# Decoder layer in float32: two more pairs of feed-forward blocks multiplied by two levels of seven products, and the weight preparation spread anew

## The chip, the cores and the metric

One core of a Trainium2 chip runs the whole layer in one launch. The metric is the device time of a launch in microseconds (us); for the kernel before it is the median of three runs.

## The reference, cut to what matters

```
x = x + attn(layernorm(x))            # one head of width 256, over each batch's 128 rows
x = x + xattn(layernorm(x), ctx)      # 8 linear-attention heads of width 64
h = layernorm(x)                      # 16 batches x 128 rows, width 1024
W = (nibble(Wq) - zero) * scale       # int4 weights, groups of 64; gate, up: 2752x1024, down: 1024x2752
x = x + (silu(h @ Wg.T) * (h @ Wu.T)) @ Wd.T
```

Everything is float32. The 2048 rows go through the feed-forward in two passes of 1024.

## The kernel before, in words

**Order of the work.** Self-attention (four groups of four batches, loop `for t in range(NT)`), cross-attention (16 batches), the feed-forward's first pass over gate and up, its second pass, and the down projection. All of it is one program; what isn't marked as kept in program order may be moved by the scheduler that builds each engine's instruction list. What goes through `InOrder` (line 53) keeps the order in which the code issues it.

**Seven products instead of eight.** The 2752 hidden units make 11 blocks of 256 (the last, number 10, has 192; `RB` is 10). A block's product of weights (256x1024) by activations (1024x1024 tokens) is cut into halves in all three dimensions and formed from seven products in place of eight (Strassen's scheme in Winograd's form). The seven left operands per matrix are sums of quarters of the dequantised weights; `prepare` (line 200) makes them on VectorE and stores them in DRAM. The right operands, called T, are sums of quarters of the activations and are made once per pass.

**One level**, `one_block` (line 1108), used for blocks 0 to 9 in the first pass: `SEQUENCE` has seven products for gate and seven for up. A product is four matmuls of 128x128 weights by 128x512 activations (`products`, line 1070, tile `p`). ScalarE copies three of the partial sums out (`k`), VectorE adds them (`sg`, `h`), and `h` is stored. PSUM banks are shared by several products: product 3 is accumulated in the bank that the sum for product 5 has just been read from, so it must wait until VectorE has read that one.

**Two levels**, `two_levels` (line 1279), used in the second pass for all five pairs of blocks: each of the seven outer products of a pair is itself formed from seven inner ones. The matmuls are 128x128 by 128x256 (tile `q`). One outer step is 7 inner products of 4 matmuls, for gate and up and both blocks at once. GpSimd forms four inner left operands (`li`) per outer step from two loaded weight tiles, VectorE forms four inner right operands (`ti`, `inner_right`, line 1228) and adds up the outer sums U, V and C (`got`, line 1325); ScalarE copies (`k`) and applies silu. Five of the seven sets of right operands are kept for all pairs (`KEPT`). VectorE's small jobs that aren't sums are queued in `soon_due` and `extra` and issued by `do_extra` (line 1291) between products.

**Preparing weights.** `prepare` is a generator. A matrix of a block takes three steps: two units (each loads 256 KB of packed weights and their scales and zeros, then six VectorE instructions on tiles `pa`) and one combination (four VectorE instructions on tiles `pc`); seven tiles of 256 KB are stored. Loads run two units ahead. Here the first three blocks' gate and up (18 steps) are prepared in self-attention (`EARLY = 3`, one load ahead), in groups 1 and 2. The other 79 steps run from block 0 of the first pass on: `beside` (line 1475) takes one step after 9 of a block's 14 products, with gate, up and down jobs mixed (`attention_done`, line 972).

**Loads and stores.** Nearly all DMAs are issued by SyncE in one queue. `load_weights` (line 1007) fetches prepared weights as tiles of 512 KB, four tiles ahead, from the list `to_load`; a tile buffer comes free when TensorE has used it. The second pass's activations (`b`, 4.2 MB) are loaded ahead of block 8.

Of the kernel before, what the change touches and what calls it, by code (L numbers as in the profile page):

```python
# [18 lines left out]
P = 128  # L19
# [46 lines left out]
def decoder_layer(  # L66
# [214 lines left out]

    EARLY = 3

# [26 lines left out]
    with (  # L310
# [166 lines left out]
        for t in range(NT):  # L477
# [14 lines left out]
            for f in range(4):  # L492
                if t == 0:
                    query_key(f, xnT, qkT, halves[f], ts(1, TB // 2))
                else:
                    query_key(f, xnT, qkT)
                add_bias(t * BPT + f)
                if more:
                    if oT is not None:
                        give((t - 1) * BPT + f, oT)  # L500
                    turn((t + 1) * BPT + f, xnTs[0])
                if more and t > 0:
                    for _ in range(1 + f % 2):
                        next(early, None)
# [15 lines left out]
            oT = attend(atT, v)  # L520
            if more and t > 0:
                for _ in range(3):
                    next(early, None)
    for _ in early:
# [437 lines left out]
    with ExitStack() as gs:  # L962
# [9 lines left out]
        def attention_done():  # L972

            nonlocal cxb, rest
            sides.close()
            prep_pools(second, "f", 6, 2)
            jobs = []
            for blk in range(EARLY, len(BLOCKS)):
                jobs += [(blk, mat) for mat in ("gu" if blk < RB else "rm")]
                if blk >= EARLY + 2:  # L980
                    jobs.append((blk - EARLY - 2, "d"))
            jobs += [(blk, "d") for blk in range(len(BLOCKS)) if (blk, "d") not in jobs]
            rest = prepare(jobs, 2, nc.sync, vector)
            banks.append(pool("c_u", 4, space=PSUM, side="right"))
            cxb = pool("c_xb", 1)

# [8 lines left out]
        def tiles_of(blk):  # L995
            todo = [(blk, *k) for k in (SEQUENCE if blk < RB else LAST)]
            return [todo[n : n + 2] for n in range(0, len(todo), 2)]

        OUTERS = [(i, q) for i in range(NI) for q in DOWN]
        to_load = deque(  # L1000
            [t for blk in range(len(BLOCKS)) for t in tiles_of(blk)]
            + [[(2 * i + f, mat, q) for mat in "gu"] for i, q in OUTERS for f in range(2)]
            + tiles_of(RB)
        )
        loaded, waiting = deque(), deque()
# [63 lines left out]

        def products(T, got):  # L1070

# [6 lines left out]
            def product(q):  # L1078
# [7 lines left out]
                for j in range(JC):  # L1086
                    nc.tensor.matmul(  # L1087
                        ps,
                        wt[:, j, :],
                        T[q][:, j, :],  # L1090
                        start=(first == q and j == 0),
                        stop=(q in (2, 3, 4) and j == JC - 1),
                        skip_group_check=True,
                    )
# [13 lines left out]
        def one_block(blk, T, between):  # L1108
# [20 lines left out]

            make = {"g": products(T, gate), "u": products(T, up)}  # L1130
            for n, (mat, q) in enumerate(SEQUENCE):
# [3 lines left out]
        def last_block(ps, T, between):  # L1135
# [24 lines left out]
            def half_product(p, w, q, start, stop):  # L1160
                for j in range(JC):
                    nc.tensor.matmul(  # L1162
                        bank[p],
# [61 lines left out]
        HT = TB // 2  # L1225
        R = {}

        def inner_right(T, q):

            if q in KEPT and (q, 7) in R:  # L1230
                return []

            def t(kc, h):
                return T[q][:, ts(kc, CHUNKS), ts(h, HT)]

            R[q, 1], R[q, 2], R[q, 3] = t(0, 0), t(1, 0), t(1, 1)

            def comb(k):
                if k == 5:
                    tag = KEPT.get(q, "ti")  # L1240
                    pool = {"ti": deep_pool, "X4": [xres]}.get(tag, [xlate])[0]
                    R[q] = pool.tile([P, 4, CHUNKS, HT], F32, name="ti", tag=tag, bufs=1)
                dst = R[q, k] = R[q][:, (5, 6, 7, 4).index(k)]
                a, b = {
                    5: (t(0, 1), t(0, 0)),
                    6: (t(1, 1), R.get((q, 5))),
                    7: (t(1, 1), t(0, 1)),
                    4: (t(1, 0), R.get((q, 6))),
                }[k]
                vector.tensor_tensor(dst, a, b, ALU.subtract)  # L1250

            return [lambda k=k: comb(k) for k in (5, 6, 7, 4)]

        def inner_left(L, pool, tag):
# [9 lines left out]
            def comb(k):  # L1264
                t = L[k] = pool.tile([P, 2, CHUNKS, P], F32, name="li", tag=tag)
                a, b, op = {
# [8 lines left out]

        deep_pool = []
        deep = ExitStack()

        def two_levels(T):
            scalar = InOrder(tc, nc.scalar)  # L1280
            deep_pool.append(
                deep.enter_context(
                    tc.tile_pool(name="c_d", bufs=1, side="right", reuse_waits="tile")
                )
            )
            wide = [P, 4, 2, HT]


            soon_due, extra = deque(), deque()

            def do_extra(n, more=0):
                for todo, k in ((soon_due, n), (extra, more)):
                    for _ in range(min(k, len(todo))):
                        todo.popleft()()
# [5 lines left out]
            def multiply(n, p):  # L1300
# [3 lines left out]
                if set_ == p:  # L1304
                    bank[p] = banks[n % 2].tile([P, 2, HT], F32, name=f"q{p}", tag="gu")
                ps = bank[set_]
                for m in range(2):
                    for c in range(CHUNKS):
                        tensor.matmul(
                            ps[:, m, :],  # L1310
                            L[p][:, m, c, :],
# [6 lines left out]
                if p in (1, 7, 6):  # L1318
                    t = state[n]["kept"][p] = ct.tile(
                        [P, 2, HT], F32, name="k", tag=f"k{p}", bufs=2 if p == 1 else 1  # L1320
                    )
                    scalar.copy(t, ps)
                put_stores()
# [27 lines left out]
            def finish(i, q):  # L1351
# [5 lines left out]
                def mult(f):  # L1357
# [3 lines left out]
                    hs[s, half, f] = t = t.rearrange("p h t -> p (h t)")  # L1361
                    if s == 1:
                        store(2 * i + f, 4, half, t)
# [20 lines left out]
            def prepare_outer(n):  # L1384
                state[n] = {"L": {}, "bank": {}, "kept": {}}

                state[n]["left"] = inner_left(
                    state[n]["L"], *((chc, "hc") if n == 0 else (ct, "sg"))
                )

# [5 lines left out]
            for n, (i, q) in enumerate(OUTERS):  # L1396
                last = n + 1 == len(OUTERS)
                if q in (1, 5):
                    sums["U" if q == 1 else "V"] = deep_pool[0].tile(
                        wide, F32, name="U" if q == 1 else "V"  # L1400
                    )
# [5 lines left out]
                multiply(n, 6)  # L1407
                do_extra(2)
                if q not in (1, 5):
                    sums["C"] = deep_pool[0].tile(wide, F32, name="C")  # L1410
                if not last:
                    soon_due.extend(inner_right(T, OUTERS[n + 1][1]))
                if n == 0:
                    extra.append(lambda: outer_operand(T, 4))
                elif n == 4:
                    extra.extend(inner_right(T, 4))
                multiply(n, 2)
                got(n, (0, 0), 2, 1)
                do_extra(1)
                multiply(n, 5)  # L1420
# [13 lines left out]
                if not last:  # L1434
                    left(3)
                do_extra(1, 1)
                load_weights()
                if not last:
                    do_extra(len(soon_due))
                    multiply(n + 1, 7)  # L1440
                if q in (2, 3, 7, 4):
                    finish(i, q)


                if q == 3:
                    while extra:
# [4 lines left out]
                elif q == 1 and i > 0 or last:  # L1451
                    do_extra(len(soon_due), len(extra))
                    hl = load_first(i if last else i - 1, 0)
                    combine(i if last else i - 1, 0, hl)
                del state[n]
            return extra

        def load_first(i, half):
# [7 lines left out]
            return hl  # L1466

        for n in range(AHEAD):

            load_weights(nc.gpsimd if n == 0 else nc.sync)  # L1470
        T = T0
        T.update({1: blocks[0, 0], 2: blocks[1, 0], 3: blocks[1, 1]})
        T1 = {}

        def beside(n, mat, q):
            if rest is None:
                tick()
                if not pend:
                    attention_done()
            elif n % 7 in (0, 2, 4, 5) or n == 6:  # L1480
                next(rest, None)

            if blk == RB:
                for k in {("r", 0): (5,), ("r", 1): (7,), ("m", 6): (6,)}.get((mat, q), ()):
                    outer_operand(T1, k)
                if (mat, q) == ("m", 1):
                    for step in inner_right(T1, 1):
                        step()

        for blk in range(len(BLOCKS)):  # L1490
            if blk == RB - 2:
                pass1 = new_blocks(cxb, lambda k: f"b{k}")
                for _ in block_loads(1, pass1):
                    pass
                T1.update({1: pass1[0, 0], 2: pass1[1, 0], 3: pass1[1, 1]})
            if blk == RB:
                blocks.update(pass1)
                last_block(0, T, beside)
            else:
                one_block(blk, T, beside)  # L1500
        for _ in rest:
            pass
        second.close()
        chc = pool("c_hc", 8)
        remaining = two_levels(T1)

# [271 lines left out]
```

## Time and profile before

| what | value |
|---|---|
| runs | 2294.47, 2295.57, 2297.4 us, median 2295.57 |
| profiled execution | 2296.27 us; span from first to last instruction 2294.5 us |
| granted TensorE clock | 0.999 |
| self-attention | 0 to 252 us |
| cross-attention | 252 to about 825 us, its end interleaved with block 0 |
| first pass, blocks 0 to 9, from 808.0 us | until the last block at 1313.6 us |
| first pass, last block | 1313.6 to 1354.8 us |
| second pass, five pairs by two levels | 1354.8 to 1779.9 us |
| second pass, last block, then the down projection | 1779.9 to 1817.6, to 2294.5 us |
| busy: TensorE, VectorE, ScalarE, GpSimd | 2269.7, 1554.0, 555.4, 389.2 us |

PE is TensorE, PEld its weight loads, DVE VectorE, ACT ScalarE, POOL GpSimd, SP SyncE. A row of instructions gives the line in the code, the engine, the operation, the tiles written and read, and their shapes; a bracket gives the idle time before it and what ended it. A line L62 is the helper that keeps the order, so tiles tell such rows apart. One float32 matmul leaves two MATMUL records. A row of a window gives the busy time of each engine in that stretch, the number of instructions in parentheses, the granted clock, the mean busy share of the 16 DMA engines and their rate.

### The profile page before, as it was taken

To read this page: it belongs to the slowest core of one execution; us is meant where nothing else is said; L and a number is where in the kernel's file an instruction comes from. 1 tells how busy PE (TensorE), PEld (TensorE's weight loads), DVE (VectorE), ACT (ScalarE), POOL (GpSimd) and SP (SyncE) were. 2 spreads that over 40 slices of the span, in tenths; PEclk is the share of its full clock that TensorE was granted. 3 is DMA by queue.
4 is the path that set the end of the run, shared out by engine and by line. 5 is a ranking of instruction groups with operands and counts; after the bars stand their busy time and mean duration, and the time that the engine had idled before them with its cause. 6 is when DMAs were issued, how large, how long until landed. Compare 5 with 4: busy or idle time off the path is not lost.

```text
span 2294.5 us, 25166 instructions
## 1 busy us (share of the span) xinstructions
PE 2269.7 (99%) x8928; PEld 1581.6 (69%) x8928; DVE 1554.0 (68%) x2210; ACT 555.4 (24%) x887; POOL 389.2 (17%) x283
## 2 busy tenths in 40 slices
PE   8999999999999999999999999999999999999999
PEld 7556566666666664444444468888888588888888
DVE  6694788788788836677776548777777655444463
ACT  2111256665665652111111111222121100000000
POOL 5120122222222210000000024444443000000000
PEclk9999999999999999999999999999999999999999
DMA  6242356566576657888789733654654974434631
GB/s 245 62 138 90 110 156 184 164 193 189 161 229 203 171 157 249 264 273 281 260 282 332 256 104 103 202 173 140 202 183 145 328 243 153 140 125 148 221 115 37
DMA packets 274797, 425.19 MB, mean 185 GB/s; under 512 B 26225, under 2 KB 119793, under 8 KB 274545
## 3 DMA queue, kind: packets, MB, share of 16 engines
q1 hardware_dynamic: 254192, 396.06, 54.5%
q10 hardware_dynamic: 18016, 18.62, 2.6%
q0 software_dynamic: 2464, 8.91, 1.0%
q8 instruction: 71, 1.16, 0.2%
q14 instruction: 54, 0.43, 0.1%
HBM read 265.62 MB, written 157.35 MB: 184 GB/s over the span
## 4 chain that ended last, share of the span: by engine, by line
PE 94%; DVE 3%; DMA 1%; issue 1%; ACT 0%; SPq 0%; POOL 0%; DVEq 0%; POOLq 0%; ACTq 0%
PE p L1087 23%; PE po L1663 21%; PE q L62 18%; PE mm L62 11%; PE kq L62 8%; PE mm L392 5%; PE tr L62 3%; PE mm L407 2%; PE mm L288 2%; PE p L1162 1%; PE tr L339 1%; DMA kh<-kd 1%; DVE bnst L62 0%; DVE qden L62 0%; DMA wo_again<-in_wo 0%
## 5 line engine op out<-in xcount | busy, mean ns | idle before, releaser
L1087 PE MATMUL p<-b,w 128*128 128x512 f32 x704 | 310.4, 592 | 0.7 <-DMA w<-wg 0.7
L1087 PEld LDWEIGHTS p<-b,w 128*128 128x128 f32 x704 | 133.4, 190 | 167.1 <-issue 162.8
L1087 PE MATMUL p<-T,w 128*128 128x512 f32 x528 | 234.2, 592 | 0.0
L62 PE MATMUL q<-ti,li 128*128 128x256 f32 x840 | 193.0, 379 | 1.0 <-DVE ti L62 1.0
L1087 PEld LDWEIGHTS p<-T,w 128*128 128x128 f32 x528 | 100.1, 190 | 124.6 <-issue 123.1
L1663 PE MATMUL po<-wc,lc 128*128 128x256 f32 x840 | 183.4, 379 | 0.0
L62 POOL TENSOR_TENSOR li<-w 128x512 f32<-128x512 f32 x70 | 96.1, 1374 | 514.6 <-DMA w<-wu 476.8
L62 PEld LDWEIGHTS q<-ti,li 128*128 128x128 f32 x840 | 159.2, 190 | 23.8 <-issue 1.7
L1663 PEld LDWEIGHTS po<-wc,lc 128*128 128x128 f32 x840 | 159.6, 190 | 21.8
L708 POOL TENSOR_TENSOR qe<-qe,qden 128x1024 f32<-128x1024 f32 x64 | 121.6, 1900 | 266.3 <-DVE qden L62 233.6
L62 ACT COPY k<-q 128x512 f32<-128x512 f32 x105 | 61.4, 585 | 324.8 <-PE q L62 324.8
L62 DVE TENSOR_TENSOR pa<-pa,sz 128x512 f32<-128x512 int32 (+1 forms) x172 | 129.0, 750 | 5.4
L1663 PE MATMUL po<-wq,lq 128*128 128x256 f32 x560 | 126.7, 379 | 0.0
L62 PE MATMUL mm<-kh,cxt 128*128 128x256 f32 x512 | 123.0, 383 | 3.3 <-DMA kh<-kd 3.1
L62 PE MATMUL kq<-cx,wk_sb 128*128 128x512 f32 x256 | 122.0, 599 | 3.5 <-ACT ke L665 3.5
L62 PEld LDWEIGHTS mm<-qs,m_sb 128*128 128x128 f32 x512 | 97.2, 190 | 38.9 <-issue 28.0
L62 PE MATMUL kq<-wq_sb,xn 128*128 128x512 f32 x256 | 120.4, 593 | 0.0
L62 PE MATMUL mm<-qs,m_sb 128*128 128x256 f32 x512 | 120.3, 379 | 0.0
L62 PEld LDWEIGHTS mm<-kh,cxt 128*128 128x128 f32 x512 | 96.1, 190 | 33.6 <-issue 18.5
L62 DVE TENSOR_REDUCE qmx<-kq 128x16 f32<-128x1024 f32 x64 | 76.3, 1193 | 63.0 <-PE kq L62 62.8
L1663 PEld LDWEIGHTS po<-wq,lq 128*128 128x128 f32 x560 | 106.0, 190 | 15.7 <-issue 0.9
L392 PE MATMUL mm<-xnT,wqkv_sb 128*128 128x512 f32 (+1 forms) x320 | 113.2, 510 | 0.0
(189 smaller groups left out, 3651.9 us busy)
## 6 DMA issues: line engine op xcount, KB each, us to landing
w<-wu SPq DMA_DIRECT2D x140, 256.0 KB, 3.5
lq<-h SPq DMA_DIRECT2D x140, 256.0 KB, 4.4
w<-wg SPq DMA_DIRECT2D x138, 256.0 KB, 3.0
kd<-kt SPq DMA_DIRECT2D x64, 512.0 KB, 3.5
kh<-kd SPq DMA_DIRECT2D x128, 256.0 KB, 5.6
h<-hc SPq DMA_DIRECT2D x80, 256.0 KB, 2.8
wq<-wd SPq DMA_DIRECT2D x70, 256.0 KB, 5.0
h<-h SPq DMA_DIRECT2D x60, 256.0 KB, 3.2
```

Of the source, the lines that this page charges most:

```text
L62: return lambda *args, **kw: self._tc.keep_in_program_order(fn(*args, **kw))
L288: tensor.matmul(ps, oT[:, d, ts(b % BPT, S)], wo_d[d][:, ts(h, 512)], start=(d == 0), stop=(d == 1),)
L339: nc.tensor.transpose(tr[:, j, :], xn[:, ts(4 * h + j, P)], ident)
L392: nc.tensor.matmul(ps[:, tokens], wqkv_sb[:, f, c, :], xnT[:, c, tokens], start=(c == 0), stop=(c == CC - 1),)
L407: nc.tensor.matmul(ps, xnT[:, c, ts(i, S)], wqkv_sb[:, 4:6, c, :], start=(c == 0), stop=(c == CC - 1),)
L708: nc.gpsimd.tensor_tensor(qe, qe, den.unsqueeze(2).to_broadcast(wide), ALU.mult)
L1087: nc.tensor.matmul(ps, wt[:, j, :], T[q][:, j, :], start=(first == q and j == 0), stop=(q in (2, 3, 4) and j == JC - 1), skip_group_check= ...
L1162: nc.tensor.matmul(bank[p], w[:, j, :], T[q][:, j, :], start=(start and j == 0), stop=(stop and j == JC - 1), skip_group_check=True,)
L1663: nc.tensor.matmul(bank[:, i, :], l[:, ts(i, S)], w,  start=(start and c == 0 and i % 2 == 0), stop=(stop and c == len(pairs) - 1), skip_g ...
```

## The change

In the first pass blocks 4 to 7 (pairs 2 and 3) go through `two_levels` between block 3 and block 8. That function now takes the pass, the pairs and an object that holds a pass's right operands. In the first pass nothing is kept: all seven sets are made for each of the two pairs, in two buffers. The order in which the four inner right operands of a set are made is 7, 5, 6, 4 instead of 5, 6, 7, 4, in the second pass too, and they have a queue of their own, `right`. Five blocks are prepared in self-attention (30 steps, now in all four groups) instead of three. The other 67 steps are 12 per one-level block (after all products but n = 3 and 10), 9 in block 3, one per pair in the two-level part, and 5 in the last block; all of gate and up comes first, then down. The second pass's activations are loaded after the two-level part. TensorE's products from block 1 on are kept in program order.

```diff
-    EARLY = 3
+    EARLY = 5
...
-                if more and t > 0:
+                if t > 0:
                     for _ in range(1 + f % 2):
                         next(early, None)
...
-            if more and t > 0:
-                for _ in range(3):
-                    next(early, None)
+            for _ in range((4, 3, 3, 2)[t]):
+                next(early, None)
...
-            jobs = []
-            for blk in range(EARLY, len(BLOCKS)):
-                jobs += [(blk, mat) for mat in ("gu" if blk < RB else "rm")]
-                if blk >= EARLY + 2:
-                    jobs.append((blk - EARLY - 2, "d"))
-            jobs += [(blk, "d") for blk in range(len(BLOCKS)) if (blk, "d") not in jobs]
+            jobs = [(blk, mat) for blk in range(EARLY, RB) for mat in "gu"]
+            down = [(blk, "d") for blk in range(len(BLOCKS))]
+            jobs += down[:4] + [(RB, "m"), (RB, "r")] + down[4:]
...
+        PAIRS = [2, 3]
+        order = [blk for blk in range(RB) if blk // 2 not in PAIRS]
+        order.insert(2 * PAIRS[0], None)
...
-            return [lambda k=k: comb(k) for k in (5, 6, 7, 4)]
+                return [lambda k=k: comb(k) for k in (7, 5, 6, 4)]
...
                 multiply(n, 6)
-                do_extra(2)
+                do_extra(len(right))
+                while soon_due:
+                    soon_due.popleft()()
...
-                    soon_due.extend(inner_right(T, OUTERS[n + 1][1]))
+                    right.extend(operands.inner_right(OUTERS[n + 1][1]))
...
                 got(n, (0, 0), 2, 1)
-                do_extra(1)
                 multiply(n, 5)
...
                     hs[s, half, f] = t = t.rearrange("p h t -> p (h t)")
-                    if s == 1:
+                    if ps == 0:
+                        store(2 * i + f, 1 + s, half, t)
+                    elif s == 1:
                         store(2 * i + f, 4, half, t)
...
-            elif n % 7 in (0, 2, 4, 5) or n == 6:
+            elif {2 * PAIRS[0] - 1: n < 9, RB: n % 2 == 0}.get(blk, n % 7 != 3):
                 next(rest, None)
...
-        for blk in range(len(BLOCKS)):
-            if blk == RB - 2:
+        for blk in order:
+            if blk is None:
+                two_levels(
+                    0, PAIRS, first_operands, lambda q: q == 1 and next(rest, None)
+                )
+                deep.close()
+                cxb = pool("c_xb", 1)
                 pass1 = new_blocks(cxb, lambda k: f"b{k}")
```

## The prediction

> **What bounds the kernel now.** The page comes first: who is busy, and what the chain that ends last is made of.
>
> ```profile
> PE 2269.7 (99%) x8928; PEld 1581.6 (69%) x8928; DVE 1554.0 (68%) x2210; ACT 555.4 (24%) x887; POOL 389.2 (17%) x283
> PE 94%; DVE 3%; DMA 1%; issue 1%; ACT 0%; SPq 0%; POOL 0%; DVEq 0%; POOLq 0%; ACTq 0%
> ```
>
> TensorE (PE) is busy 99% of the span and is 94% of the chain. Only fewer or shorter matmuls can gain; everything else can only lose. So the question is what TensorE saves, and which cover the change uses up. Windows by stage show the cover: first a one-level block, then block 8 with the second pass's activations, then one pair by two levels.
>
> ```profile
> 1010.00:1061.00 51.00, 51.00 (x120) 22.58 (x119) 37.66 (x64) 6.59 (x11) 0.00 (x0) 1.00 0.83 277
> 1213.00:1263.00 50.00, 50.00 (x118) 22.07 (x117) 35.63 (x59) 6.01 (x10) 0.00 (x0) 1.00 1.03 348
> 1525.00:1610.00 85.00, 85.00 (x396) 74.82 (x395) 63.43 (x83) 16.71 (x26) 37.18 (x28) 1.00 0.53 175
> ```
>
> After the total come PE, PEld, DVE, ACT and POOL; the last two numbers are the DMA share and GB/s. In a one-level block VectorE (DVE) is 74% busy and the DMAs 83%; near block 8 the DMAs are full. TensorE waits nowhere, at a granted clock of 1.00.
>
> **What TensorE saves.** The timeline of PE, at the change from one level to two and at the end of the second pass's pairs:
>
> ```profile
> 1341.08 3.60 PE L1087 MATMUL p<-b,w 128*128 128x512 f32 x8
> 1344.52 7.03 PE L1087 MATMUL p<-T,w 128*128 128x512 f32 x16
> 1351.38 3.60 PE L1087 MATMUL p<-b,w 128*128 128x512 f32 x8
> 1354.82 1.89 PE L62 MATMUL q<-b,w 128*128 128x256 f32 x8
> ```
> ```profile
> 1779.85 7.03 PE L1162 MATMUL p<-b,w 128*128 128x512 f32 x16
> ```
>
> Starts count, since records overlap, and a matmul has two records. From 1341.08 to 1354.82 us there are 32 records, 16 wide matmuls in 13.74 us: 0.859 each, 3.44 a product, 48.1 a block. From 1354.82 to 1779.85 us lie all 980 narrow ones: 0.4337 us each, with the pass's own waits, 85.0 a pair. The two instruction lists hold 648 and 424 matmuls of tile p, 980 and 1372 of tile q, and the rest of PE's list is the same; so the change does what it says. Gone are 224 x 0.859 = 192.4 us, new 392 x 0.4337 = 170.0: **22.4 us less**. PE's weight loads go from 44% to 88% of such a stretch, and the last pairs ran so without a gap.
>
> **Self-attention: 12 more steps on VectorE.** Rows of one-level blocks price a step:
>
> ```profile
> L62 DVE TENSOR_TENSOR pa<-pa,sz 128x512 f32<-128x512 int32 (+1 forms) x20 | 13.8, 692 | 0.7
> L62 DVE TENSOR_SCALAR pa<-raw 128x512 int32<-128x512 int32 x13 | 5.5, 419 | 0.0
> L62 DVE TENSOR_TENSOR pc<-pa 128x512 f32<-128x512 f32 x7 | 4.8, 686 | 0.1
> ```
>
> A unit is 2 x 419 + 4 x 692 ns = 3.61 us, a combination 4 x 686 = 2.74, a matrix of three steps 9.95. Four matrices more are 39.8 us. Four steps (13.6 us) go to the end of group 0, where VectorE waits 10.1 us until 73.35 and 4.9 us more until 107; they fit, barely. Eight go to group 3 (about 26 us), where the trace has 22.6 us of idle time and then gaps:
>
> ```profile
> 222.07 0.42 DVE L414 TENSOR_TENSOR v<-mm,bv_sb 128x256 f32<-128x256 f32 x1 [22.59 <-PE mm L407]
> ```
> ```profile
> 250.36 0.10 DVE L62 SCALAR_TENSOR_TENSOR shift<-mv,rstd 128x1 f32<-128x1 f32 x1
> 254.40 1.23 DVE L62 TENSOR_REDUCE knmax<-kq 128x1 f32<-128x1024 f32 x1 [3.94 <-PE kq L62]
> 257.10 0.69 DVE L62 TENSOR_TENSOR X<-mm,X 128x512 f32<-128x512 f32 x1 [1.47 <-PE mm L62]
> 258.82 1.23 DVE L62 TENSOR_REDUCE qmx<-kq 128x16 f32<-128x1024 f32 x1 [1.02 <-PE kq L62]
> ```
>
> In the new list the last unit and combination, 6.35 us, stand right before `shift` at 250.36, which then runs at about 256.6; queued behind are `knmax`, `qmx` and `qe`, for which ScalarE and then TensorE wait. The gaps here are 3.94 + 1.47 + 1.02 = 6.43 us, so some 1 us is passed on; VectorE is then busy 29.4 of 30 us from 270 to 300 and won't catch up there. The stores and loads of these steps find a queue that is under half busy from 40 to 250 us. I take **1.5 us**; the ends are 0 and 9 (the burst passed on whole, and 2.7 us, a combination, in group 0).
>
> **Two levels in the first pass.** The new list makes all right operands for both pairs, four `ti` of 0.68 to 0.82 us per outer step; in return the `hc` combinations are absent. The tight step is outer product 7. In the second pair of the second pass VectorE worked through it without a gap from 1507.09 to 1518.99 us, while PE began the next step's product 6 at 1519.12. Three `ti` (2.0 us) now stand before that product, which needs the third of them: about 0.6 us late, twice. The prepare step after outer product 1 (3.61 us) falls into a light step. Entry: both tiles for `li` are loaded four tiles, 27 us, ahead, and VectorE has no steps after n = 8 of block 3. Against that the new order may win back the 1.0 us that TensorE waited for `ti` in the second pass. I take **1 us**; the ends are -1 and 11 (0.82 us lost in each of 14 steps).
>
> **One-level blocks 1, 2, 8, 9: 12 steps in place of 9.** This cover is used up. Four matrices are 39.8 us, the block's own ten sums of 0.69 us are 6.9: 46.7 of 48.1 us by durations (74 instructions at the 0.588 us of the first window give 43.5). VectorE must not be late by more than product 4 lasts, 3.44 us, since product 3 overwrites the bank that the sum for product 5 reads. No step follows the product before product 5 (n = 3, 10), so VectorE is on time there if it never waits for a DMA. Does it?
>
> - Blocks 1 and 2: 14 weight loads and 4 stores of 262 KB, and 2.62 MB a matrix: 15.2 MB in 48.1 us, 316 GB/s.
> - Blocks 8 and 9: counted in SyncE's new list 19.7 MB (with 4.2 MB of activations at the front) and 18.4 MB, 396 GB/s.
>
> The DMA view from 1216 to 1294 us has every slice full:
>
> ```profile
> DMA  9999999999999999999999999999999999999999
> DMA packets 12917, 26.96 MB, mean 346 GB/s; under 512 B 1765, under 2 KB 1765, under 8 KB 12912
> ```
>
> 346 GB/s covers blocks 1 and 2, not 8 and 9: 38.1 MB take 110.1 us, 13.9 us over the blocks' 96.2. Before, VectorE had 13 us of slack per block; now 1.4 to 4.6. Against this stand loads two units and four tiles ahead, VectorE's slack and TensorE's 3.44 us; and the light last block, with 5 steps, takes what is still queued. The ends are 0 and 13.9. I take **4 us**, nearer to nothing, since in the full stretch VectorE waited only 4.3 us in all for DMAs.
>
> A rule bears on that ceiling: the Trainium skill, "DMA: Bandwidth & Descriptors", section "Where 436 GB/s comes from", names about 358 GB/s as a core's share of HBM and 435 as the fabric's limit. By the first the two blocks would be an estimated 10 us late, by the second not at all; the stretch above is nearer to the first, against the change.
>
> **The sum.** 22.4 - 1.5 - 1 - 4 = 15.9 us less than the profiled execution's 2296.27: 2280.4. That execution is 0.7 us above the median, so the median after should be near **2280**.
>
> **Rivals.**
> - *All covers hold.* Self-attention and the steps lose at most 2 us in all and the `ti` waits vanish: 2272 to 2276. For it: PE lost no time in the full stretch. Against: VectorE's slack is nearly gone. Chance 0.20.
> - *The forecast*, losses of 3 to 13 us: 2276 to 2286. Chance 0.50.
> - *DMAs decide blocks 8 and 9.* The 13.9 us come through, with 2 to 5 elsewhere: 22.4 - 18 = about 4 to 9 us less, 2286 to 2291. For it: a full queue and steps that VectorE must take in order. Chance 0.18.
> - *The gain is just eaten*: 2291 to 2300, the last case with 5 us more in self-attention and in the first pass's `ti`. Chance 0.06.
> - *Slower, by unit waits.* Each unit waits w for its packed weights, VectorE reaches the sum for product 5 late, and TensorE stands at product 3. With 8 units a block and 1.4 us of slack, four blocks lose 4 x (8w - 1.4); beside 2.5 us elsewhere that passes 19.9 from w = 0.8 us on. At w = 1.5 it is 42.4: 2318. For it: these loads landed after 5.6 us in the full stretch, 4.9 over the whole run. Against: waits there came to under 0.1 us a unit. Chance 0.06.
>
> The range goes from 2273 to 2290; about 0.2 lies outside. Faster by over 0.2% (below 2291, about what a measurement of this kernel can tell) is 0.20 + 0.50 + 0.18 = 0.88; same 0.06; slower 0.06.
>
> **What would show it.** PE's stretch for blocks 4 to 7 takes 170 to 172 us; if over 175, `ti` waits were mis-sized. `shift` starts near 256 us, and cross-attention is 1 to 2 us later. Blocks 1 and 2 take 48 us each; blocks 8 and 9 together 96 to 103, with PE idle at product 3 and VectorE waiting for DMAs. The down projection is unchanged. I am wrong if blocks 1 and 2 stretch too, or if blocks 8 and 9 pass 110 us.

## The result, and the profile after

After the change the median is 2305.03 us (2302.85 to 2309.31, five runs) against 2295.57 us: a ratio of 1.0044, 95% interval 1.0029 to 1.0058. The layer became 9.5 us slower where the prediction had it 15.6 us faster. The first lines of the page, busy times and the chain that ended last:

```profile
PE 2257.3 (98%) x9264; PEld 1648.9 (72%) x9264; DVE 1681.7 (73%) x2340; ACT 564.7 (25%) x899; POOL 467.9 (20%) x339
PE 87%; DVE 7%; DMA 3%; issue 2%; ACT 1%; SPq 0%; POOL 0%; DVEq 0%; POOLq 0%; ACTq 0%
```

TensorE is busy 12.4 us less, not 22.4, in part because it ran at half clock for 30.7 us of this execution, where a matmul takes longer (below). Its share of the chain fell from 94% to 87%: it waits now. The starts of PE's first matmul of each stage, differences in us, from the two profiled executions:

| stage | before | after | after less before |
|---|---|---|---|
| start to the first one-level product | 808.0 | 817.8 | +9.8 |
| blocks 0 to 3 | 220.7 | 221.2 | +0.6 |
| blocks 4 to 7 | 192.3 | 178.0 | -14.2 |
| block 8 | 48.1 | 48.1 | 0 |
| block 9 | 48.1 | 55.0 | +6.9 |
| last block, first pass | 37.8 | 41.6 | +3.8 |
| second pass and down projection, to the span's end | 939.7 | 941.6 | +1.9 |

(The differences are taken before rounding; they add up to that of the spans, 2303.3 - 2294.5 = 8.8.) What TensorE waited for, in the view of waits (total, times, longest):

```profile
PE mm L62 <- DMA wo_again<-in_wo: 9.9, 2, 8.2
PE tr L339 <- ACT xn L147: 9.3, 1, 9.3
PE q L62 <- DVE ti L62: 6.6, 4, 2.8
PE p L62 <- DVE h L62: 5.8, 2, 3.9
```

The second row is the start of the kernel and old. Before, the first was 0.4 us, the third 1.0 us, and the fourth wasn't there. Three windows of the changed kernel answer to those of before: block 2, the first pair of the first pass, and block 9.

```profile
942.00:990.00 48.00, 48.00 (x114) 21.21 (x112) 44.18 (x75) 6.01 (x10) 0.00 (x0) 1.00 0.96 317
1039.00:1128.00 89.00, 86.22 (x392) 75.30 (x391) 67.33 (x85) 15.87 (x25) 35.81 (x27) 0.98 0.45 145
1265.00:1320.00 55.00, 51.06 (x113) 22.21 (x112) 44.90 (x75) 5.89 (x10) 0.00 (x0) 0.94 1.04 314
```

In block 2 the DMAs move 317 GB/s and TensorE waits nowhere, though VectorE is busy 44.2 of 48 us. In the other two TensorE has idle time, and the granted clock is below 1.00.

**The seam.** SyncE's queue where self-attention ends and cross-attention begins (start, length):

```profile
245.82 1.09 SPq L650 DMA_DIRECT2D cx<-in_cx  x2
253.28 0.33 SPq L209 DMA_DIRECT2D wu<-pa  x1
254.01 2.25 SPq L209 DMA_DIRECT2D wu<-pc  x4
...
257.35 0.40 SPq L868 DMA_DIRECT2D wo_again<-in_wo  x1
...
259.11 0.43 SPq L868 DMA_DIRECT2D wo_again<-in_wo  x1
```

After `cx` the queue stands still for 6.4 us: its next entries are the stores of VectorE's last unit and combination, which VectorE only finishes at 255.9. The loads of `wo_again`, which need nothing from VectorE, are queued behind them; before, they were issued right after `cx`, at 247.56. On PE:

```profile
251.51 1.98 PE L62 MATMUL kq<-cx,wk_sb 128*128 128x512 f32 x4
261.70 2.05 PE L62 MATMUL mm<-wo_again,oT 128*128 128x512 f32 x2 [8.20 <-DMA wo_again<-in_wo]
265.43 2.08 PE L62 MATMUL mm<-wo_again,oT 128*128 128x512 f32 x2 [1.68 <-DMA wo_again<-in_wo]
```

The granted clock is 0.50 from 257.8 us for 13.65 us. (Two matmul records take 2.05 us here; four took 2.29 us before.) The last wait that the seam brings, for `ke`, ends on PE at 299.87 us before and at 312.01 us after, so the seam costs 12.1 us; 2.4 of them come back later (experiment 2).

```profile
299.87 1.98 PE L62 MATMUL kq<-cx,wk_sb 128*128 128x512 f32 x4 [1.08 <-ACT ke L665]
```
```profile
312.01 1.98 PE L62 MATMUL kq<-cx,wk_sb 128*128 128x512 f32 x4 [1.08 <-ACT ke L664]
```

**Outer product 7.** PE, VectorE and GpSimd in the first pair:

```profile
1113.32 1.89 PE L62 MATMUL q<-ti,li 128*128 128x256 f32 x8
1117.99 3.63 PE L62 MATMUL q<-ti,li 128*128 128x256 f32 x8 [2.78 <-DVE ti L62]
```
```profile
1111.69 0.68 DVE L62 TENSOR_TENSOR ti<-T 128x512 f32<-128x512 f32 x1
...
1113.73 1.72 DVE L62 TENSOR_TENSOR C<-C,V 128x512 f32<-128x512 f32 x1
1115.37 1.75 DVE L62 TENSOR_TENSOR ti<-T 128x512 f32<-128x512 f32 x1
1117.15 0.69 DVE L62 TENSOR_TENSOR ti<-T,ti 128x512 f32<-128x512 f32 x1
```
```profile
1113.63 1.27 POOL L62 TENSOR_TENSOR li<-w,li 128x512 f32<-128x512 f32 x1 [3.14 <-PE q L62]
1115.30 1.27 POOL L62 TENSOR_TENSOR li<-w 128x512 f32<-128x512 f32 x1 [0.40 <-PE q L62]
```

VectorE is busy throughout, and two of its instructions, both while GpSimd makes an `li`, take 1.7 us in place of 0.7. The third `ti` ends at 1117.8, and TensorE has waited 2.78 us.

**Block 9.** VectorE before TensorE's wait of 3.94 us, which ends at 1313.91:

```profile
1293.55 1.42 DVE L62 TENSOR_TENSOR pa<-pa,szd 128x512 f32<-128x512 int32 x2 [1.85 <-DMA szd<-in_dsz]
...
1306.33 0.43 DVE L62 TENSOR_SCALAR pa<-raw 128x512 int32<-128x512 int32 x1 [1.50 <-DMA raw<-in_dq]
1308.73 1.42 DVE L62 TENSOR_TENSOR pa<-pa,szd 128x512 f32<-128x512 int32 x2 [1.98 <-DMA szd<-in_dsz]
...
1311.86 0.68 DVE L62 TENSOR_TENSOR h<-p,k 128x512 f32<-128x512 f32 x1
```

Units wait for their scales; the sum for product 5, `h`, stands behind them, and product 3 waits for that bank.

### The profile page after: what moved, and what is told of

The parts are those of the page before. It is cut to its first block, busy times and chain, and to the rows that moved or that the text cites. A ratio compares the mean times of both kernels' runs of the same rounds, so it can differ in the third digit from the quotient of the medians.

```text
span 2303.3 us, 26140 instructions
## 1 busy us (share of the span) xinstructions
PE 2257.3 (98%) x9264; PEld 1648.9 (72%) x9264; DVE 1681.7 (73%) x2340; ACT 564.7 (25%) x899; POOL 467.9 (20%) x339
## 4 chain that ended last, share of the span: by engine, by line
PE 87%; DVE 7%; DMA 3%; issue 2%; ACT 1%; SPq 0%; POOL 0%; DVEq 0%; POOLq 0%; ACTq 0%
PE q L62 24%; PE po L1700 20%; PE mm L62 11%; PE p L62 10%; PE kq L62 8%; PE mm L392 5%; PE tr L62 3%; PE mm L407 2%; PE mm L288 2%; PE p L1087 2%; DVE pa L62 1%; DMA szd<-in_dsz 1%; PE tr L339 1%; DMA kh<-kd 1%; DVE ti L62 1%
## 5 line engine op out<-in xcount | busy, mean ns | idle before, releaser
L62 PE MATMUL q<-ti,li 128*128 128x256 f32 x1176 | 274.3, 383 | 6.6 <-DVE ti L62 6.6
L62 PEld LDWEIGHTS q<-ti,li 128*128 128x128 f32 x1176 | 225.1, 192 | 39.8 <-issue 7.1
L62 POOL TENSOR_TENSOR li<-w 128x512 f32<-128x512 f32 x98 | 133.2, 1361 | 353.6 <-DMA w<-wu 155.7
L62 ACT COPY k<-q 128x512 f32<-128x512 f32 x147 | 86.1, 586 | 468.2 <-PE q L62 468.2
L62 PE MATMUL p<-b,w 128*128 128x512 f32 x432 | 194.8, 604 | 6.1 <-DVE h L62 5.8
L62 PEld LDWEIGHTS p<-b,w 128*128 128x128 f32 x432 | 83.4, 194 | 112.4 <-issue 100.1
L62 PE MATMUL p<-T,w 128*128 128x512 f32 x304 | 134.7, 592 | 0.0
L62 PEld LDWEIGHTS p<-T,w 128*128 128x128 f32 x304 | 57.8, 190 | 72.7 <-issue 72.0
```

Source lines behind the costliest of these rows:

```text
L62: return lambda *args, **kw: self._tc.keep_in_program_order(fn(*args, **kw))
```

## The experiments

Theory: three separate causes (queue order at the seam, VectorE at outer product 7, steps late in a full DMA queue in block 9 and the last block), and a half-speed clock behind each long wait. "Changed" is 2305.03 us; the kernel before had 2296.0 to 2296.4 us beside these runs.

**1. `early_only`: the kernel before with the self-attention part alone** (`EARLY = 5`, the `if t > 0`, and `(4, 3, 3, 2)[t]`).

> The kernel before, with only the self-attention part of the change (five blocks prepared there, the same steps at the same places). Theory (queue): `wo_again` stands in SyncE's queue behind the last five stores, which wait for VectorE's last combination, so TensorE waits some 8 to 10 us at 252 to 267 us and the granted clock halves behind it; nothing else is changed, so the time is 2295.6 + 9.9 = about 2305 us, and the first one-level block starts near 818 us. Rival (the record's term): only VectorE's burst is passed on, 1.5 us, 2297 us. Second rival: the seam costs 10 us only beside the other parts of the change; then this kernel is near 2296.

2306.18 us, ratio 1.0041 (1.0026 to 1.0055). The first one-level product starts at 816.8, and blocks 1 to 9 take 48.1 us each. TensorE waits 7.65 and 2.71 us for `wo_again`. This part alone makes the kernel about 10 us slower; all the rest of the change together is worth nearly nothing.

**2. `wo_queue`: three loads on another queue.**

```diff
-            nc.sync.dma_start(wo_again[d], wo[ts(d, P)])
+            nc.gpsimd.dma_start(wo_again[d], wo[ts(d, P)])
```
(`xbo_sb` and `gs_sb` likewise.)

> The changed kernel, with the loads of `wo_again`, `xbo_sb` and `gs_sb` issued by GpSimd in place of SyncE; VectorE's list is the same. Theory (queue): the waits of 8.2 and 1.7 us go, the clock stays at 1.00 from 258 to 271 us, the first one-level block starts at 808 to 811 us and the time falls by 7 to 10 us, to about 2296 us. Rival (VectorE): the two steps of 6.35 us that stand before `shift` are what delays TensorE, whatever queue the loads are in; then at most 2 us come back, 2303 us or more.

2294.52 us, ratio 0.9993 (0.9984 to 1.0002); first one-level product at 808.6. GpSimd issues the loads at once, while VectorE still has its two steps to do:

```profile
250.65 1.55 POOL L868 DMA_DIRECT2D wo_again<-in_wo  x2
```
```profile
255.50 0.68 DVE L62 TENSOR_TENSOR pc<-pa,pc 128x512 f32<-128x512 f32 x1
256.72 0.15 DVE L62 TENSOR_SCALAR gs_sb<-gs_sb 128x1 f32<-128x1 f32 x1 [0.54 <-DMA gs_sb<-in_xg]
```

The clock did not stay at 1.00 as expected: TensorE still waits once, and the clock is 0.50 from 255.88 to 259.29 us.

```profile
256.31 3.45 PE L62 MATMUL mm<-wo_again,oT 128*128 128x512 f32 x4 [2.52 <-ACT g_sb L646]
```
```profile
302.57 1.98 PE L62 MATMUL kq<-cx,wk_sb 128*128 128x512 f32 x4 [1.08 <-ACT ke L664]
```

At the wait for `ke` this kernel stands at 302.57 us, against 299.87 before and 312.01 in the changed kernel: the place of the three loads in the queue (they were moved together) costs 9.4 of the seam's 12.1 us. `best` below, which moves VectorE's two steps as well, stands at 300.74, so the burst costs 1.8. That the first one-level product starts only 0.6 us later than before is mostly the clock's doing: the kernel before waits 2.16 us for `kh` at 697 us and runs at half clock behind it, while this one and the changed one wait 1.40 and 1.47 us there and keep their clock. In the view of before:

```profile
700.39:703.80 3.41, 3.41 (x7) 1.69 (x6) 1.16 (x2) 0.00 (x0) 0.00 (x0) 0.50 1.07 396
```

**3. `busy`: TensorE kept at work while it waits.**

```diff
+        def keep_busy():
+            ps = btr.tile([P, 512], F32, name="idle", tag="tr")
+            for n in range(9):
+                tensor.matmul(ps, wk_sb[:, :P], wq_sb, start=True, stop=True)
+        later(1, keep_busy)
```

> The changed kernel, with nine matmuls of 128x512 whose product is not used, put on TensorE right before the first matmul that waits for `wo_again` (9 x 0.859 = 7.7 us, inside the wait of 8.2 us). The wait stays. Theory (the halved clock is a cost of its own): the clock stays at 1.00 up to 271 us, and the work of some 8 us that ran at half speed takes 4 us less: about 2301 us, the first one-level block near 814 us. Rival (the clock figure goes with the idle time and costs nothing beside it): the time stays at 2305 us or rises with the added matmuls.

2302.77 us, ratio 1.0026 (1.0016 to 1.0035), the first one-level product at 817.1.

```profile
254.30 7.89 PE L62 MATMUL idle<-wq_sb,wk_sb 128*128 128x512 f32 x18
262.03 1.02 PE L62 MATMUL mm<-wo_again,oT 128*128 128x512 f32 x2
266.22 2.08 PE L62 MATMUL mm<-wo_again,oT 128*128 128x512 f32 x2 [3.17 <-DMA wo_again<-in_wo]
```

The first matmul on `wo_again` now ran at full speed (1.02 us, not 2.05), but then TensorE waited for the second load, to 266.2 as against 265.4. The start at 817.1 lies within the 816.7 to 818.8 us of the seven executions in which the seam wasn't edited, so nothing clear came back there, and the interval overlaps that of the changed kernel. My 4 us were wrong: up to 266 us the second load sets the pace, not the clock.

**4. `seam_steps`: the last two steps a group earlier.**

```diff
-            for _ in range((4, 3, 3, 2)[t]):
+            for _ in range((4, 4, 4, 0)[t]):
```

> The changed kernel, with the last two steps of self-attention moved from the end of group 3 to the ends of groups 1 and 2 (4, 4, 4, 0 in place of 4, 3, 3, 2). Theory (queue) and the VectorE rival both expect that the waits at the seam go: 7 to 10 us less there. A further rival: groups 1 and 2 have no room on VectorE for a step of 2.7 to 3.6 us more each, so that 3 to 6 us come back as TensorE's waits before 250 us; by the theory alone 2296 us, by this one 2299 to 2302 us.

2295.26 us, ratio 0.9992 (0.9982 to 1.0002); first one-level product at 809.3, no new wait before 250 us. The stores are then through before the loads come, so this and `wo_queue` take the same loss away from two sides.

**5. `ti_first`.**

> The changed kernel, with three of the four `ti` of the next outer product put on VectorE before the sum that follows product 3, in place of after it (first pass only). Theory (VectorE's order): the `ti` that product 6 of the next step waits for is then ready 2 us or more earlier, the gaps of 2.78 and 2.22 us at 1118 and 1207 us and the half clock behind each (1.71 us lost each) go: 8 us less in the stretch of blocks 4 to 7, 170 in place of 178 us, time about 2297 us. Rival (VectorE and GpSimd together have not the time for outer product 7): the wait only moves to another product, and the stretch stays above 175 us.

2304.18 us, ratio 1.0040 (1.0025 to 1.0055), waits of 2.78 and 2.22 us as before. The edit left VectorE's list as it was: its three `ti` already stood there. It says nothing on the theory, but as a repeat it showed the clock. The first pair took 87.6 us in place of 89.3, though the wait was the same. The 3.4 us behind that wait, in the changed kernel and in this one (the value before the DMA share is the clock):

```profile
1118.00:1121.40 3.40, 3.40 (x8) 2.77 (x9) 2.81 (x5) 1.06 (x1) 0.00 (x0) 0.50 0.00 0
```
```profile
1119.00:1122.40 3.40, 3.40 (x16) 3.01 (x17) 2.82 (x4) 1.53 (x2) 1.27 (x1) 1.00 0.00 0
```

Eight records in the one, sixteen in the other: half the clock for 3.4 us costs 1.7 us. Of the seven executions with this wait (2.77 to 3.28 us) it follows in five; the wait of 2.2 us in the second pair it follows in all seven. The last section says why.

**6. `spread`: four steps from block 9 and the last block into the pairs.**

```diff
-            elif {2 * PAIRS[0] - 1: n < 9, RB: n % 2 == 0}.get(blk, n % 7 != 3):
+            elif {2 * PAIRS[0] - 1: n < 9, 9: n % 7 not in (2, 3), RB: n % 4 == 0}.get(blk, n % 7 != 3):
...
-                    0, PAIRS, first_operands, lambda q: q == 1 and next(rest, None)
+                    0, PAIRS, first_operands, lambda q: q in (1, 2, 5) and next(rest, None)
```

> The changed kernel, with four preparation steps taken from block 9 (two) and the last block (two) and put behind outer products 2 and 5 of both pairs, where the DMA queue is half empty. Theory (VectorE late from steps that wait in a full queue): the wait of 3.94 us at product 3 of block 9 shrinks below 2 us and that of 1.87 us in the last block goes, and with them their half-clock stretches; blocks 8, 9 and the last together 135 to 138 in place of 144.6 us, time 2297 to 2300 us. Rival (the pairs have no room): the stretch of blocks 4 to 7 grows by as much, from 178 to 184 us, and the time stays.

2305.22 us, ratio 1.0046 (1.0029 to 1.0063). The rival held: block 9 took 48.1 in place of 55.0 us, but the pairs 188.0 in place of 178.0. The last block kept its wait (1.88 us); it took 39.9 us only because no half clock followed. The step behind outer product 2 alone brings three waits:

```profile
1071.65 1.99 PE L62 MATMUL q<-ti,w 128*128 128x256 f32 x8 [0.72 <-DVE ti L62]
...
1076.14 1.97 PE L62 MATMUL q<-T,li 128*128 128x256 f32 x8 [0.77 <-DVE C L62]
...
1082.14 1.10 PE L62 MATMUL q<-ti,li 128*128 128x256 f32 x4 [2.31 <-DVE ti L62]
```

**7. `no_sz`: fewer bytes, the same VectorE work** (`szd` loaded for one unit only, so that all others are scaled with its values).

> The changed kernel, with scale and zero of the down projection's weights loaded once, for the first unit, and used again by all others (the packed weights then get a wrong scale: that part of the computation is changed). VectorE's instructions stay the same; the DMA load falls by about 1 MB a matrix of `d`, in blocks 8 and 9 from 38 to some 30 MB. Theory (a full DMA queue makes VectorE late): VectorE's waits for DMAs at 1289 to 1309 us go, TensorE's waits of 3.94 and 1.87 us with them, and blocks 8, 9 and the last take 134 to 136 in place of 144.6 us; time about 2296 us. Rival (VectorE's own load of 46.7 of 48.1 us): the waits of TensorE stay, 142 us or more.

2294.73 us, ratio 0.9996 (0.9987 to 1.0005); block 9 48.1 us, last block 37.8, as before the change. The window of block 9, to be held against the third one of the changed kernel above:

```profile
1265.00:1320.00 55.00, 55.00 (x130) 24.39 (x129) 50.76 (x87) 6.59 (x11) 0.00 (x0) 1.00 0.90 309
```

VectorE does even more in it (50.8 us, more instructions got done) and TensorE waits nowhere. So VectorE had the time; it was the transfers that made it late. The edit takes away bytes and a number of transfers at once; which of the two counts wasn't separated.

**8. `all_four`: edits 2, 4, 5 and 6 together.**

> The changed kernel with four edits together: `wo_again`, `xbo_sb` and `gs_sb` on GpSimd's queue, the last two steps of self-attention one group earlier, three `ti` before the sum that follows product 3, and four steps moved from block 9 and the last block into the pairs. Theory (the four waits with their half-clock stretches took the gain): seam 8 to 10, pairs 7 to 8, blocks 9 and last 6 to 9 us less than the changed kernel, 2305 - 24 = about 2281 us, faster than both. Rival (the waits turn into one another, since VectorE's time is used up): at least half of it stays, 2293 us or more.

2294.77 us, ratio 0.9994 (0.9985 to 1.0004), some 14 us more than the theory gave. The seam (806.0) and block 9 (48.1) are mended; the pairs take 188.0, so edit 6 pays with one hand what it takes with the other, and edit 5 does nothing.

**9. `ti_kept`: the set for outer product 4 made once, in block 3.**

```diff
...
-        first_operands, second_operands = Operands(T, {}), Operands(T1, KEPT)
+        first_operands, second_operands = Operands(T, {4: "X6"}), Operands(T1, KEPT)
...
-            if blk == 2 * PAIRS[0] - 1 and n == 9:
-                for step in first_operands.inner_right(DOWN[0]):
+            if blk == 2 * PAIRS[0] - 1 and n in (9, 11):
+                for step in first_operands.inner_right({9: DOWN[0], 11: 4}[n]):
```

> The changed kernel, with the four `ti` for outer product 4 made once, at n = 11 of block 3, and kept in a tile that is free in this pass (that of X6), so that VectorE has no `ti` to make during outer product 7 of either pair. Theory (VectorE is late at that step, by the `ti` and by what GpSimd's `li` beside it costs): the waits of 2.78 and 2.22 us go, with the half clock that follows them in some executions (1.7 us each); the pairs take 170 to 172 us in place of 176.4 (without the half clock) to 178.0, time 5 to 8 us less than the changed kernel: 2297 to 2300 us. Rival (the 16 sums of that step alone already fill VectorE): a wait of 1 us or more stays at 1117 and 1206 us.

2297.13 us, ratio 1.0004 (0.9995 to 1.0013). The pairs take 84.6 us each, 169.2, with no wait.

**10. `no_li`: GpSimd silent in the pairs** (the `li` of the first outer product used by all, so that blocks 4 to 7 are computed from the wrong weights).

> The changed kernel, with the left combinations `li` of the first pass's pairs made only for the first outer product and used again by the other 13 (so h of blocks 4 to 7 is computed from wrong weights). GpSimd is then idle in the pairs; VectorE's list is the same. Theory (VectorE's instructions with both operands in SBUF stand still while GpSimd reads SBUF: 1.72 for 0.69 us, 1.75 for 0.68, 2.37 for 1.29 for two): at outer product 7 VectorE gains 3.5 us, the waits of 2.78 and 2.22 us go, pairs 170 to 172 us, time 5 to 8 us less: 2297 to 2300 us. Rival (the long durations have another cause, such as waiting for the bank or for the load of the DMA queue): these instructions stay long and the waits stay above 1.5 us.

2297.73 us, ratio 1.0007 (0.9998 to 1.0017); pairs 169.2 us, no wait. VectorE at the same place:

```profile
1112.60 0.69 DVE L62 TENSOR_TENSOR C<-C,V 128x512 f32<-128x512 f32 x1
1113.21 0.68 DVE L62 TENSOR_TENSOR ti<-T 128x512 f32<-128x512 f32 x1
1113.92 0.69 DVE L62 TENSOR_TENSOR ti<-T,ti 128x512 f32<-128x512 f32 x1
```

The same two instructions now take 0.69 and 0.68 us in place of 1.72 and 1.75. Experiments 9 and 10 remove the wait from two sides: fewer `ti` or a silent GpSimd. VectorE is late only by both together.

**11. `six`: six blocks in self-attention** (`EARLY = 6`, 9 steps each in blocks 8 and 9, and edit 2).

> The changed kernel with six blocks prepared in self-attention (36 steps: two more beside group 0's query and key products, then 5, 6, 5 and 0 at the ends of the groups), so that blocks 8 and 9 have 9 steps each as before the change, and with the loads of `wo_again`, `xbo_sb` and `gs_sb` on GpSimd's queue. Theory (blocks 8, 9 and the last lose their time to a full DMA queue): 6.8 MB less there, 134 to 136 us in place of 144.6; and if VectorE's idle time before 250 us (38 us) can be used, the first one-level block still starts at 806 to 810 us: time 2284 to 2288 us. Rival (the idle time lies where a step can't use it): TensorE waits 5 to 15 us more before 250 us, and the time is 2290 to 2300 us.

2297.31 us, ratio 1.0007 (0.9997 to 1.0016). Blocks 8, 9 and the last take 133.9 us, so all of the loss there is gone; but the first one-level product starts at 817.8 again:

```profile
63.81 1.09 PE L452 MATMUL tr<-ident,at 128*128 128x128 f32 x4 [5.38 <-DVE at L444]
```

A wait of 3.68 us at 196 us is the other. The rival held: TensorE waits 9.1 us more before 250 us, each time for VectorE's `at`. That a step put into VectorE's idle time delays its answer to TensorE there is the likely reading, not tested by itself. Another distribution wasn't tried.

**12. `best`: edits 2, 4 and 9, and four steps behind outer products 6 and 5** (`q in (1, 6, 5)`; last block n = 0, 1, 8).

> The changed kernel with what the runs so far point to: the three loads on GpSimd's queue and the last two self-attention steps one group earlier (first one-level block at 806 in place of 817.8 us), the `ti` for outer product 4 kept in X6's tile (pairs 169.2 in place of 178.0 us), and four steps taken from block 9 and the last block and put behind outer products 6 and 5, before which VectorE had 3.3 us of idle time (block 9 back from 55.0 to 48.1 us; the three that stay in the last block at n = 0, 1 and 8, last block 38 to 40 in place of 41.6 us). Theory (the waits are separate and each has its cause taken away): 11.9 + 8.8 + 6.9 + 2 to 4 + 1 less, and 0 to 2 us lost again in the pairs: 2305 - 29 = about 2276 us, 0.8% faster than the kernel before. Rival (steps beside outer products 6 and 5 make TensorE wait as they did behind 2 and 5, 2.5 us each): 2284 to 2288 us.

2279.22 us (2277.6 to 2282.59), ratio 0.9925 (0.9911 to 0.9939): faster than both.

```profile
PE 2250.1 (99%) x9264; PEld 1646.3 (72%) x9264; DVE 1683.7 (74%) x2336; ACT 564.7 (25%) x899; POOL 476.5 (21%) x343
```
```profile
PE q L62 <- DVE ti L62: 4.3, 5, 2.1
...
PE mm L62 <- DMA wo_again<-in_wo: 1.1, 1, 1.1
```

First one-level product 808.4, pairs 86.6 each, blocks 8, 9 and the last 48.1, 48.1 and 37.8. Against the 29 us hoped for, the median fell by 25.8. In the profiled execution, the slowest of the five (2282.59 us), the seam gave 9.4 of 11.9 us, the pairs 4.8 of 8.8 (86.6 for 84.6 each), and the second pass lost 2.5 in place of winning 1 (a wait of 2.10 us at its start and a half clock).

## Why the prediction was wrong

Its own steps, with what the runs give in their place:

- **TensorE's saving**: 22.4 us. The pairs without waits take 169.2 us (experiments 9 and 10) for 192.3: 23.1. Right.
- **Self-attention**: 1.5 us, upper end 9. It was 9.8. The step that failed is "The stores and loads of these steps find a queue that is under half busy from 40 to 250 us". A queue's fill was read where its order mattered: SyncE issues in order, and a store that waits for VectorE holds every load behind it. VectorE's burst, which the step did price, cost 1.8 us at the seam (experiment 2), so "some 1 us is passed on" was roughly right. That only 9.8 of the seam's 12.1 us show is luck: the kernel before lost 2.4 us at 697 to 704 us that the new one didn't.
- **Two levels in the first pass**: 1 us, upper end 11. It was 178.0 - 169.2 = 8.8. The step that failed is "PE began the next step's product 6 at 1519.12", and with it "about 0.6 us late, twice". In the rows of before, products 7 and 6, which both read `ti` and `li`, are the 16 records of the first row below, so product 6 began at 1517.39; the row at 1519.12 reads `T` and `w` and is product 2.

```profile
1515.67 3.62 PE L62 MATMUL q<-ti,li 128*128 128x256 f32 x16
1519.12 1.89 PE L62 MATMUL q<-T,w 128*128 128x256 f32 x8
```

  With the right start the prediction's own sum (1517.71 + 2.0) gives 2.3 us late in place of 0.6; the waits were 2.78 and 2.22 us. The rest was mis-sized too: one of the three `ti`, beside GpSimd's `li`, takes 1.75 us in place of 0.68, and the half clock behind each wait took 1.7 us more.
- **Blocks 1 and 2**: 48.1 us each, as forecast. 317 GB/s is carried.
- **Blocks 8, 9 and the last**: 4 us, ends 0 and 13.9. It was 10.7 (144.6 against 133.9 in experiments 7 and 11). The mechanism was right (a full queue, units waiting, product 3 standing), the size wasn't: "nearer to nothing, since in the full stretch VectorE waited only 4.3 us" was read with 9 steps a block, when VectorE had 13 us of slack to hide its waits in. Block 8 lost nothing: the slack and the loads ahead lasted for it, not for block 9. Blocks 8 and 9 together took 103.0 us, the upper end of the sign given for them (96 to 103); the last block with its five steps was no refuge, it lost 3.8 us.
- **The clock**: no term at all. "TensorE waits nowhere, at a granted clock of 1.00" was taken as a constant, though the trace of before has its own half-clock stretch at 700.39 us, behind a wait. It is a result of not waiting: each long wait can cost 1.7 to 2.7 us on top. Counted where it can be separated, the pairs lost 3.4 us, block 9 about 2.7 (clock at 0.50 from PE's return at 1313.91 to 1319.35), the last block 1.7.
- The other 2.5 us lie in block 3, in the second pass (waits for `ti` of 0.95 and 0.61 us, where before had 1.0 in all) and in a pause of 0.87 us in the down projection.

23.1 - 9.8 - 8.8 - 10.7 - 2.5 = -8.7. Every loss lay near the upper end of its bounds or, at the seam, just beyond it; the forecast took the values near zero, and as if they were independent. That they share a cause, VectorE's and the queue's slack used up in all three places at once, is argued here, not shown: each had its own cure. The rival "The gain is just eaten" (2291 to 2300, 0.06) had the right list of places; "Slower, by unit waits" named a wait that did come, but in block 9 and the last block only, and mostly for the scales.

## What to carry to other kernels

Moving work off the bound engine uses up the cover of the others: price each spot where that cover is thinnest, with the neighbours' instructions running beside, and not from a row of the same instruction alone. When stores are added to an in-order queue, list what is queued behind each store and when the engine that produces its data will be done: a load that needs nothing may stand there, and another queue is a cheap cure. When products are told apart in a row of a profile, check by the operands which one the row is: one misread start hid 1.7 us of lateness here. A change that looks worthless can be a good one with faults at a few places: here 9.5 us slower became 17 us faster (2296.2 to 2279.2) with four small edits.

## What the runs showed of the hardware

**Waits shorter than a clock window can halve the clock, and where they fall decides.** In each of the 14 profiled executions, from 20 us on, the starts and ends of all half-clock stretches lie on one grid of 3.413 us, to within 0.001 us (where in the program a grid line falls differs from execution to execution). Laid over TensorE's idle time, the grid shows which waits cost the clock: of 43 windows at full clock with 1.87 us of idle time or more, 41 were followed by half clock (the two others had 2.00 and 2.01 us); of some 9,200 with 1.86 us or less, none was. At half clock the clock stayed there behind a window with 0.79 us of idle time or more and came back behind one with 0.44 us or less. (Ends of matmuls are modelled in the trace, so the last hundredth is uncertain.) The last block's wait of 1.84 to 1.88 us for `h` occurred in nine executions. In three it lay within one window with 1.87 or 1.88 us, a stretch of 3.41 us at 0.50 followed, and the block took 41.6 us; in four it came to 1.86 us and in two the grid split it, and the block took 39.9. The wait of 2.77 us in the first pair was split in `busy` and `ti_first` (1.59 + 1.18 us in the latter), and no half clock followed. The Trainium skill, "TensorE: Matmul & The Clock Gate", section "What's actually happening", has the clock at half after at least one idle window of about 3.4 us, in a window that runs free. The length of 3.41 us and the grid agree; that a full idle window is needed does not: 1.87 us was enough here. By that rule only the waits of 8.2 and 3.94 us could have cost the changed kernel anything beyond themselves.

**VectorE beside GpSimd.** Instructions with both operands in SBUF took 1.72 and 1.75 us beside an `li`, 0.69 and 0.68 when GpSimd was silent; the sum that reads a PSUM bank (`C<-q,k`) stayed at 0.69. The Trainium skill, "SBUF — State Buffer", section "Who interferes with whom", says just that of two SBUF inputs against a GpSimd instruction that reads SBUF. The trace agrees: the loss, 1.03 and 1.07 us, is nearly the `li`'s 1.27.

**A full DMA queue by itself did no harm.** In `six` the DMAs were at 1.03 of their time from 1245 to 1295 us (the end of block 8 and the start of block 9) and TensorE waited nowhere; VectorE was busy only 36.7 of 50 us, where in block 9 of the changed kernel, at 1.04, it was busy 44.9 of 55:

```profile
1245.00:1295.00 50.00, 50.00 (x118) 22.18 (x117) 36.68 (x62) 6.49 (x11) 0.00 (x0) 1.00 1.03 311
```
